# Four blocks of a graph layer begun ahead of the branch that chooses its form

## The chip, the cores and the metric

The kernel runs on one core of one Trainium2 chip. A core has a matrix engine (TensorE, PE in the profile, with its weight loads as PEld), a vector engine (VectorE, DVE), a scalar engine (ScalarE, ACT), a general engine (GpSimd, POOL) and a sync engine (SyncE, SP) that issues the transfers here. Each engine has its own queue of instructions and takes them in order; semaphores make one wait for another. Transfers bring data from memory (HBM) to the on-chip buffer (SBUF), and matmuls write to a small accumulator memory of eight banks (PSUM), which VectorE and ScalarE can read. The metric is the device time of one execution in microseconds.

## The reference

Four graph layers follow each other on 3327 nodes with 64 features; all use the same dense 3327 x 3327 adjacency, and after each comes a residual addition and a layer normalisation:

```python
x = _layernorm(x + _L0_gnn_ref(x, adj, L0_gnn_W), axis=-1)               # mean of neighbours, then a matmul
x = _layernorm(x + _L1_gnn_ref(x, adj, L1_gnn_weight, L1_gnn_bias), axis=-1)  # hyperbolic: see below
x = _layernorm(x + _L2_gnn_ref(x, adj, L2_gnn_W, L2_gnn_b), axis=-1)     # mean with itself, matmul, relu, unit norm
x = _layernorm(x + _L3_gnn_ref(x, adj, L3_gnn_weight, L3_gnn_bias), axis=-1)  # rank of each neighbour weights it
```

Layer 1 needs a value for every pair of nodes:

```python
w = adj / deg
log_ij = _logmap(x[:, None, :], x[None, :, :], c)
agg = jnp.einsum('ij,ijc->ic', w, log_ij)
transformed = agg @ weight + bias
```

Layer 3 weights a neighbour by its rank in the row (a running count of the nonzero entries), so those ranks must be counted from the adjacency somewhere.

## The kernel before

The nodes are padded to 3328: 26 blocks of 128 source nodes (NB) by four chunks of 832 target nodes (CH), taken in the order 0, 3, 1, 2 (ORDER). The adjacency is stored transposed and comes in pairs of blocks, 128 x 2 x 832 numbers, 832 KB, into four buffers in turn (`load_adj`, L274, issued by SP). A chunk has 13 pairs.

Layer 0 (L626 to L745) goes through each chunk's pairs from 12 down to 0. `aggregate_pair` (L434, matmul at L439) adds a pair to the chunk's sums in one PSUM bank. For three of the four chunks the ranks for layer 3 are counted on the way: `Ranks.mask` (L457) makes a 0/1 mask on VectorE (L459), and `count` (L496) sums it along the nodes with three groups of four matmuls (L505) into two PSUM pairs and lets ScalarE write the ranks (L515). The counts of a pair need a row from the pair before: `carry` (L483) takes it from that pair's result and subtracts it in the mask (L491, VectorE). So counts wait in a list, and `left` (L711) says how many stay in it: three in the last two chunks. What is left is counted after the last pair (L740).

At the end of a chunk `keep_sums` (L424) copies the sums to SBUF, `sums0` (L542) transposes them (L549) and takes degree, mean and residual on VectorE, and `features0` (L572) makes the normalised features xr, their scaled form xu, and a doubled copy `twice` (POOL) that `transposes0` (L611) turns into the operands ut and wt of layer 1. For three chunks this is done beside the next chunk's pairs, step by step (`side`). For the last one only `sums0` is, and `features0` is left for layer 1 (`late`).

Layer 1 has two forms. The short one (`layer1_far`) holds if no node lies near the origin; it is chosen at run time. Each chunk notes its near nodes; at the end VectorE adds them up (`nearest`, L742), a one-element matmul gives the count (the vote, L744), VectorE writes it as an integer (`n_near`, L745), and every engine loads it and branches (L1369, L1371). PSUM is handed over there: layer 0's pool of tiles is closed and each arm opens its own.

`layer1_far` (L785) takes 104 steps, one for each block in each chunk. `far_v` (L789) makes two matmuls (L793) into one of three PSUM pairs; `far_factors` (L801) computes p from it and the adjacency on VectorE (L804) and a square on ScalarE, then a product of both: either ScalarE, ScalarE, POOL (L817, L818, L819, form G) or ScalarE, VectorE (L809, L812, form V), in the pattern GVGGGV. `far_aggregate` (L822, L824) multiplies the result s with xu into the chunk's sums, six steps behind (L1_AHEAD). Groups of two steps are issued together: two `far_v`, their factors, then two aggregations. From step 3 on (LATE_AT) one step of the last group's `features0` is put behind each block's p, and then its transposes.

The first two adjacency pairs of layer 1 have a place of their own: the buffer `sums`, whose halves are free once the groups in them are transposed. SP issues both loads after all of layer 0's pairs (L734).

TensorE's order is written out by hand: `issue_after` puts an instruction behind another in the program order without making it wait; where no such order is given, the framework's scheduler orders each engine's program.

Of the kernel before, what the change touches and what calls it, by code (L numbers as in the profile page):

```python
# [79 lines left out]


# [15 lines left out]
LATE_AT = 3  # L97
# [11 lines left out]
def four_gnn_layers_kernel(  # L109
# [516 lines left out]
    with ExitStack() as l0s:  # L626
# [60 lines left out]

        heads = {12: (24, 26), 11: (20, 24), 9: (13, 20), 6: (6, 13), 2: (0, 6)}
# [5 lines left out]
        for n, c in enumerate(ORDER):  # L694
# [4 lines left out]
            for jp in reversed(range(NB // 2)):  # L699
# [11 lines left out]
                left = (L0_SPILL - jp // 2 if ranks else jp // 2) if n < 2 else L0_LAG  # L711
# [3 lines left out]
                if side is not None and jp < NB // 2 - 1:  # L715
                    on_array = jp == NB // 2 - 2
                    if not step(side, (counted or issued) if on_array else mask if ranks else None):
                        side = None
                        transposes0(ORDER[n - 1], places.free(), counted or issued, True)
                        if n == NCH - 1:  # L720

                            nc.scalar.activation(nothing, wt[:, GROUPS[ORDER[n - 1]][0] * P].unsqueeze(1), AF.Tanh)
# [6 lines left out]
            if n < NCH - 1:  # L729
                side = finish0(c, banks.one(n % 2))  # L730
            else:
                last_group = all_of(sums0(c, banks.one(n % 2)))

        first_pairs = [  # L734
            load_adj(ORDER[0], PAIRS[k], sums[:, bass.ts(k, 2 * CH)].rearrange(
                "p (b i) -> p b i", b=2
            ))
            for k in range(2)
        ]
        count(masked, places, 0, counted)  # L740
        nearest = small.tile([P, 1], FP, name="nearest", tag="nearest")
        nc.vector.tensor_reduce(nearest, near, axis=AX.X, op=ALU.add)  # L742
        vote = banks.one(NCH % 2)
        nc.tensor.matmul(vote[0:1, 0:1], lhsT=nearest, rhs=ones, start=True, stop=True)  # L744
        nc.vector.tensor_copy(n_near, vote[0:1, 0:1])  # L745
# [39 lines left out]
    def layer1_far(banks, begin2):  # L785

        with tc.tile_pool(name="l1w", bufs=1) as wp:

# [105 lines left out]
            for start in range(0, total + L1_AHEAD, L1_GROUP):  # L894
                group = range(start, start + L1_GROUP)
                made = []
                for i in group:
                    if i < total:
                        if i % 2 == 0:
                            c, jp, a2 = next(pairs)  # L900
                        jb = 2 * jp + i % 2
                        v, v_issued = far_v(c, jb, summed)
                        made.append((i, jb, v, a2[:, i % 2, :]))
# [38 lines left out]
                for i in group:  # L942
                    n, j = divmod(i - L1_AHEAD, NB)
# [485 lines left out]
```

## Time and profile before

| | us |
|---|---|
| median of 3 runs | 538.31 (537.72 to 540.17) |
| the profiled execution, its own time | 536.65 |
| its span, first to last instruction | 534.9 |
| TensorE, VectorE, ScalarE, POOL busy | 484.1, 389.5, 334.1, 176.2 |
| last aggregation of layer 0 (pair 0), start | 141.84 |
| n_near written | 152.21 |
| first layer 1 matmul, first layer 1 aggregation | 153.88, 165.50 |
| last aggregations of layer 1 end, about | 345.9 |

The profile shows one execution. Times in it count from its first instruction. Each line of a time line is a run of equal instructions on one engine: start, time from the first start to the last end, engine, line of the source, operation, what is written and read, the size, how many, and in brackets how long the engine stood idle before it and which instruction ended the wait. An adjacency pair's aggregation is eight rows of L439, since every fp32 matmul leaves two rows; a block's `far_v` is four rows of L793.

### The profile page before, as it was taken

Reading aid. Unit: us, or ns where it says so; the run is one execution under the profiler, and the core shown is the slowest. Engines: PE = TensorE matmul, PEld = TensorE weight load, DVE = VectorE, ACT = ScalarE, POOL = GpSimd, SP = SyncE. Lnnn points to the kernel's source line nnn. Section 1 sums busy time; section 2 is a strip of 40 time slices with the busy share of each in tenths; the row PEclk is TensorE's granted clock in tenths of the full one; section 3 lists DMA queues with packets and bytes.
Section 4 is the critical chain, followed back from the end, with each engine's and each line's share of the span. In section 5 each row is a group of like instructions: output and inputs, shape, how many; then the busy total and the mean of one; then the engine's idle time right before and its main releaser. Section 6 shows DMA issues by size and latency. Waiting matters only on the chain.

```text
span 534.9 us, 8471 instructions
## 1 busy us (share of the span) xinstructions
PE 484.1 (90%) x3256; PEld 242.7 (45%) x3256; DVE 389.5 (73%) x707; ACT 334.1 (62%) x393; POOL 176.2 (33%) x150
## 2 busy tenths in 40 slices
PE   5999999998858999998999999997798999999993
PEld 3555444454423334433443353352344675656672
DVE  3575449899669888799789869945699972736834
ACT  1436536786868989788879977500278653236931
POOL 2001101112008888767767875221022020210000
PEclk9999999999989999999999999999999999999997
DMA  8899999899266777767767876879997789980012
GB/s 271 308 363 347 394 399 387 297 317 305 82 229 219 254 257 260 247 208 242 244 201 256 255 227 244 290 227 355 349 320 263 234 288 325 309 319 2 1 28 43
DMA packets 47172, 135.93 MB, mean 254 GB/s; under 512 B 6903, under 2 KB 7007, under 8 KB 47059
## 3 DMA queue, kind: packets, MB, share of 16 engines
q1 hardware_dynamic: 46594, 134.75, 73.6%
q0 software_dynamic: 384, 0.52, 0.4%
q8 instruction: 27, 0.44, 0.4%
q14 instruction: 23, 0.18, 0.1%
q10 hardware_dynamic: 144, 0.03, 0.0%
HBM read 134.27 MB, written 0.85 MB: 253 GB/s over the span
## 4 chain that ended last, share of the span: by engine, by line
PE 49%; DVE 27%; ACT 10%; DMA 6%; issue 3%; POOL 1%; ACTq 0%; POOLq 0%; DVEq 0%
PE one L439 14%; PE two L1263 10%; DVE p L804 7%; PE two L793 6%; DMA adj<-in_adjt_dram 6%; DVE mask L491 5%; PE one L824 5%; PE two L505 5%; DVE s L812 4%; DVE mask L459 3%; ACT s L817 3%; PE two L439 2%; ACT s L818 2%; ACT rank L515 2%; PE two L1187 1%
## 5 line engine op out<-in xcount | busy, mean ns | idle before, releaser
L819 POOL TENSOR_TENSOR s<-s,p 128x832 f32<-128x832 f32 x67 | 130.1, 1956 | 73.3 <-ACT s L818 61.4
L804 DVE SCALAR_TENSOR_TENSOR p<-two,adj 128x832 f32<-128x832 f32 x100 | 101.0, 1018 | 17.8 <-issue 13.3
L793 PE MATMUL two<-uw 64*128 64x416 f32 x416 | 90.1, 545 | 14.3 <-DVE s L812 7.2
L515 ACT ACTIVATE rank<-two,last_bias 128x832 uint8<-128x832 f32 x78 | 71.6, 952 | 45.5 <-DVE mask L491 22.8
L824 PE MATMUL one<-s,xu 128*64 128x416 f32 x416 | 85.2, 524 | 0.0
L439 PE MATMUL one<-adj,x0w 128*64 128x416 f32 x416 | 82.3, 523 | 2.3 <-ACT x0w L644 1.4
L817 ACT ACTIVATE s<-two,far_bias 128x832 f32<-128x832 f32 x67 | 63.7, 950 | 22.7 <-DVE p L804 20.7
L439 PE MATMUL one<-adj,xr 128*64 128x416 f32 x312 | 73.3, 515 | 3.1 <-DMA adj<-in_adjt_dram 3.1
L491 DVE SCALAR_TENSOR_TENSOR mask<-two,minus_last,mask 32x832 bf16<-32x832 f32 x48 | 52.5, 1093 | 24.4 <-PE two L505 20.0
L459 DVE TENSOR_SCALAR mask<-adj 128x1664 bf16<-128x1664 f32 x52 | 55.3, 1066 | 18.8 <-DMA adj<-in_adjt_dram 18.2
L793 PEld LDWEIGHTS two<-uw 64*128 64x128 f32 x416 | 37.5, 189 | 67.0 <-PE one L824 22.6
L1263 PE MATMUL two<-bits,parts 128*64 128x416 bf16 x624 | 67.7, 339 | 0.0
L505 PE MATMUL two<-mask,tri 128*64 128x416 bf16 x416 | 53.5, 346 | 10.9 <-DVE mask L491 8.3
L818 ACT ACTIVATE s<-s 128x832 f32<-128x832 f32 x67 | 60.1, 897 | 1.9
L1263 PEld LDWEIGHTS <-parts 128*64 128x64 bf16 x624 | 41.9, 110 | 20.4 <-issue 5.0
L824 PEld LDWEIGHTS one<-s,xu 128*64 128x64 f32 x416 | 25.8, 136 | 47.5 <-issue 46.6
L505 PEld LDWEIGHTS <-tri 128*64 128x64 bf16 x416 | 24.6, 110 | 45.9 <-issue 24.9
L439 PEld LDWEIGHTS one<-adj,x0w 128*64 128x64 f32 x416 | 29.4, 138 | 34.1 <-issue 23.5
L812 DVE SCALAR_TENSOR_TENSOR s<-two,p 128x832 f32<-128x832 f32 x37 | 37.6, 1016 | 3.0 <-ACT two L809 2.5
L439 PEld LDWEIGHTS one<-adj,xr 128*64 128x64 f32 x312 | 29.4, 137 | 22.4 <-issue 13.6
L1243 ACT ACTIVATE bits<-rank 128x1664 uint16<-128x1664 uint8 x21 | 32.3, 1579 | 9.9 <-PE two L1263 9.8
L809 ACT ACTIVATE two<-two,far_bias 128x832 f32<-128x832 f32 x37 | 34.0, 919 | 5.1 <-DVE p L804 4.9
(235 smaller groups left out, 453.0 us busy)
## 6 DMA issues: line engine op xcount, KB each, us to landing
adj<-in_adjt_dram SPq DMA_DIRECT2D x152, 832.0 KB, 5.6
sums<-in_adjt_dram SPq DMA_DIRECT2D x2, 832.0 KB, 6.0
uw<-in_adjt_dram SPq DMA_DIRECT2D x2, 832.0 KB, 6.5
uw<-in_xt_dram SPq DMA_DIRECT2D x1, 640.0 KB, 10.7
last_a<-in_adjt_dram POOLq DMA_DIRECT2D x4, 84.5 KB, 7.4
out_dram<-o SPq DMA_DIRECT2D x1, 224.0 KB, 3.7
uw<-in_xt_dram SPq DMA_DIRECT2D x1, 192.0 KB, 3.2
out_dram<-o SPq DMA_DIRECT2D x1, 192.0 KB, 2.3
```

What stands on the lines that cost most here:

```text
L439: issued = nc.tensor.matmul(acc[h * D : (h + 1) * D, 0:HC], lhsT=x[:, 2 * jp + k, 0:D], rhs=a2[:, k, bass.ts(h, HC)], start=(first and k = ...
L459: issued = nc.vector.tensor_scalar(mask, a2, 0.0, None, op0=ALU.not_equal)
L491: nc.vector.scalar_tensor_tensor(halves(last), ranks.after[P - 32 : P, :, 0:HC], minus_last[P - 32 : P, :], halves(last), op0=ALU.mult, op ...
L505: issued = nc.tensor.matmul(counts[k][rows, h, 0:HC], lhsT=lhsT[:, rows], rhs=mask[:, of, bass.ts(h, HC)], start=lhsT is tri, stop=(k == 1 ...
L515: nc.scalar.activation(halves(ranks.rank[:, 2 * jp + k, :]), counts[k][:, :, 0:HC], AF.Relu, bias=last_bias,)
L793: issued = nc.tensor.matmul(v[:, h, 0:HC], lhsT=wt[rows, bass.ts(jb, P)], rhs=ut[rows, bass.ds(c * CH + h * HC, HC)], start=True, stop=True,)
L804: issued = nc.vector.scalar_tensor_tensor(halves(p), v, 0.25 - 0.5 * FD, halves(a), op0=ALU.add, op1=ALU.mult)
L817: nc.scalar.activation(halves(s), v, AF.Square, bias=far_bias, scale=-2.0)
L818: nc.scalar.activation(s, s, AF.Copy, bias=FG)
L819: nc.gpsimd.tensor_mul(s, s, p)
L824: issued = nc.tensor.matmul(acc[h * D : (h + 1) * D, 0:HC], lhsT=xu[:, jb, 0:D], rhs=s[:, bass.ts(h, HC)], start=first, stop=last,)
L1263: issued = nc.tensor.matmul(acc3[c][h * D : (h + 1) * D, 0:HC], lhsT=parts[:, 2 * jp + b, bass.ts(part, D)], rhs=bits[:, b, bass.ts(h, HC) ...
```

## The change

Three things change.

1. In the last chunk of layer 0 fewer counts wait: `left` falls from 3 to 2 at pair 4 and to 1 at pair 1, so two counts move ahead of the last pairs and one is left for the end.
2. The first four blocks of layer 1 (L1_THERE) are begun in layer 0. The first `sums` load is issued behind pair 2's load. Block 0's matmuls follow the last pair; its p goes in place over the adjacency in `sums` (VectorE), and Square, Copy and product run on ScalarE and POOL. Block 1 follows the transposes of the last group, and its p stands behind `nearest` on VectorE, ahead of the `n_near` copy. The matmuls of blocks 2 and 3 stand behind the vote, and their p and s (form V) behind the `n_near` copy, ahead of each engine's branch.
3. In `layer1_far` steps 0 to 3 make nothing and only queue the finished blocks. Blocks 0 to 3 are aggregated in steps 4 to 7, none in 8 and 9, and from step 10 on the order is as before. `LATE_AT` becomes 4. The ScalarE table load for Tanh is tied to pair 4 and another operand.

The blocks' arithmetic is the same.

```diff
+L1_THERE = 4
...
-LATE_AT = 3
+LATE_AT = 4
...
+        first_pairs = []
+        first_s = l0.tile([P, CH], FP, name="first_s")
+
+        def load_first(k):
+            there = sums[:, bass.ts(k, 2 * CH)].rearrange("p (b i) -> p b i", b=2)
+            return load_adj(ORDER[0], PAIRS[k], there)
+
+        def first_v(k, place, behind):
+            jb = 2 * PAIRS[k // 2] + k % 2
+            for h in range(2):
+                rows = slice(h * D, (h + 1) * D)
+                issued = nc.tensor.matmul(
+                    place[:, h, 0:HC], lhsT=wt[rows, bass.ts(jb, P)],
+                    rhs=ut[rows, bass.ds(ORDER[0] * CH + h * HC, HC)], start=True, stop=True,
+                )
+                issue_after(issued, behind)
+            return issued
+
+        def first_p(k, place, behind):
+            a = halves(first_pairs[k // 2][:, k % 2, :])
+            issued = nc.vector.scalar_tensor_tensor(
+                a, place[:, :, 0:HC], 0.25 - 0.5 * FD, a, op0=ALU.add, op1=ALU.mult
+            )
+            if behind is not None:
+                issue_after(issued, behind)
+
+        def first_aside(k, place):
+
+            nc.scalar.activation(
+                halves(first_s), place[:, :, 0:HC], AF.Square, bias=far_bias, scale=-2.0
+            )
+            nc.scalar.activation(first_s, first_s, AF.Copy, bias=FG)
+            a = first_pairs[0][:, k, :]
+            nc.gpsimd.tensor_mul(a, first_s, a)
...
-                left = (L0_SPILL - jp // 2 if ranks else jp // 2) if n < 2 else L0_LAG
+                if n < 2:
+                    left = L0_SPILL - jp // 2 if ranks else jp // 2
+                else:
+                    left = L0_LAG if n == 2 else min(L0_LAG, (jp + 4) // 3)
+                if n == NCH - 1 and jp == 2:
+                    first_pairs.append(load_first(0))
+                if n == NCH - 1 and jp == 0:
+                    places_v = [places.zero()]
+                    issued = first_v(0, places_v[0], issued)
+                    first_p(0, places_v[0], mask)
+                    first_aside(0, places_v[0])
                 counted = count(masked, places, left, issued)
...
-                        if n == NCH - 1:
-
-                            nc.scalar.activation(nothing, wt[:, GROUPS[ORDER[n - 1]][0] * P].unsqueeze(1), AF.Tanh)
+                if n == NCH - 1 and jp == 4:
+
+                    b0 = GROUPS[ORDER[n - 1]][0]
+                    nc.scalar.activation(nothing, om[:, b0 : b0 + 1], AF.Tanh)
...
-        first_pairs = [
-            load_adj(ORDER[0], PAIRS[k], sums[:, bass.ts(k, 2 * CH)].rearrange(
-                "p (b i) -> p b i", b=2
-            ))
-            for k in range(2)
-        ]
-        count(masked, places, 0, counted)
+        first_pairs.append(load_first(1))
+        places_v.append(places.zero())
+        issued = first_v(1, places_v[1], counted)
+        counted = count(masked, places, 0, issued)
         nearest = small.tile([P, 1], FP, name="nearest", tag="nearest")
-        nc.vector.tensor_reduce(nearest, near, axis=AX.X, op=ALU.add)
+        issued = nc.vector.tensor_reduce(nearest, near, axis=AX.X, op=ALU.add)
+        first_p(1, places_v[1], issued)
+        first_aside(1, places_v[1])
         vote = banks.one(NCH % 2)
-        nc.tensor.matmul(vote[0:1, 0:1], lhsT=nearest, rhs=ones, start=True, stop=True)
-        nc.vector.tensor_copy(n_near, vote[0:1, 0:1])
+        voted = nc.tensor.matmul(vote[0:1, 0:1], lhsT=nearest, rhs=ones, start=True, stop=True)
+        issue_after(voted, counted)
+        known = nc.vector.tensor_copy(n_near, vote[0:1, 0:1])
+
+        places_v += [places.zero(), places.one()]
+        for k in (2, 3):
+            first_v(k, places_v[k], voted)
+            first_p(k, places_v[k], known)
+        for k in (2, 3):
+            v, a = places_v[k][:, :, 0:HC], halves(first_pairs[1][:, k % 2, :])
+            nc.scalar.activation(v, v, AF.Square, bias=far_bias, scale=-2.0)
+            nc.vector.scalar_tensor_tensor(a, v, FG, a, op0=ALU.add, op1=ALU.mult)
...
+            def summed_at(i):
+
+                if i < 2 * L1_THERE:
+                    return i - L1_THERE
+                return i - L1_AHEAD if i >= L1_THERE + L1_AHEAD else -1
...
+                        if i < L1_THERE:
+                            waiting.append((jb, a2[:, i % 2, :]))
+                            continue
...
-                    n, j = divmod(i - L1_AHEAD, NB)
+                    n, j = divmod(summed_at(i), NB)
```

## The prediction

> **What bounds the kernel now.** I read the page's busy shares and slices first (TensorE, PE, is busy 90% of the 534.9 us span), then the time line of each engine around the branch, since every edit lies between 117 and 180 us of the trace. TensorE's line there:
>
> ```profile
> 128.62 1.56 PE L439 MATMUL one<-adj,x0w 128*64 128x416 f32 x8
> ...
> 130.85 0.54 PE L505 MATMUL two<-mask,tri 128*64 128x416 bf16 x4 [0.31 <-DVE mask L491]
> ...
> 134.03 1.56 PE L439 MATMUL one<-adj,x0w 128*64 128x416 f32 x8
> ...
> 138.31 1.62 PE L439 MATMUL one<-adj,x0w 128*64 128x416 f32 x8
> ...
> 141.84 1.59 PE L439 MATMUL one<-adj,x0w 128*64 128x416 f32 x8
> ...
> 151.98 0.19 PE L744 MATMUL one<-ones,nearest 128*1 128x1 f32 x2
> 153.88 3.92 PE L793 MATMUL two<-uw 64*128 64x416 f32 x12 [1.71 <-ACT rank L515]
> ...
> 165.50 1.62 PE L824 MATMUL one<-s,xu 128*64 128x416 f32 x8
> ```
>
> L439 x8 is one adjacency pair's aggregation; 141.84 is pair 0, the last of layer 0, 128.62 is pair 4. L744 is the vote, the first L793 is layer 1, the first L824 its first aggregation. So from the end of layer 0's aggregation to the start of layer 1's, 143.2 to 165.5, TensorE is half idle. The first L793 waits not for the vote but for the last ScalarE (ACT) rank, which still reads layer 0's PSUM.
>
> VectorE's (DVE) line of the same stretch:
>
> ```profile
> 134.15 1.03 DVE L459 TENSOR_SCALAR mask<-adj 128x1664 bf16<-128x1664 f32 x1 [1.17 <-DMA adj<-in_adjt_dram]
> ...
> 145.64 0.17 DVE L552 COPY deg<-one 128x7 f32<-128x7 f32 x1
> ...
> 151.34 0.18 DVE L742 TENSOR_REDUCE nearest<-near_nodes 128x1 f32<-128x26 f32 x1
> 152.21 0.14 DVE L745 CAST n_near<-one 1x1 int32<-1x1 f32 x1 [0.69 <-PE one L744]
> 155.85 1.02 DVE L804 SCALAR_TENSOR_TENSOR p<-two,sums 128x832 f32<-128x832 f32 x1 [3.49 <-PE two L793]
> ...
> 162.54 1.02 DVE L804 SCALAR_TENSOR_TENSOR p<-two,adj 128x832 f32<-128x832 f32 x1 [0.56 <-POOL s L819]
> ```
>
> n_near is known at 152.35. L804 at 155.85 is block 0's p, the one at 162.54 is block 4's: the first block that the change leaves to layer 1. And the stretches' clock (columns: length, busy time and count of PE, PEld, DVE, ACT, POOL, then granted clock, DMA share, GB/s):
>
> ```profile
> 150.20:153.60 3.40, 1.08 (x12) 0.45 (x10) 1.40 (x4) 2.78 (x4) 0.00 (x0) 1.00 0.00 0
> 153.60:157.00 3.40, 3.12 (x10) 1.85 (x12) 1.02 (x1) 0.22 (x2) 0.00 (x0) 0.51 0.71 252
> 200.00:337.00 137.00, 130.06 (x678) 54.75 (x676) 117.15 (x192) 116.76 (x140) 101.97 (x53) 1.00 0.72 238
> ```
>
> After a stretch with 1.08 us of matmul in 3.40 the clock is halved for one such stretch; it made the first twelve L793 take 3.92 us where four take 0.97 (2.9 for twelve), so about 1.0 us is lost already before. In the last row layer 1's body has TensorE busy 95%: a start-up gained or lost is carried to the end.
>
> **What the skill says.** "TensorE: Matmul & The Clock Gate", Part 1: the clock is set by a free-running window of 3413 ns, and one idle window halves it; the two rows agree in the length, and show that 1.08 us busy in 3.40 still counts as idle. "PSUM — Partial Sum Buffer", PSUM bank collisions: two engines may not touch one bank together, reads included, so accesses are ordered; agrees: rank L515 is released by DVE L491, at 148.72 right at its end. "DMA: Bandwidth & Descriptors", Anatomy of one DMA: about 2 us fixed plus the bytes, stated for the GpSimd path; the SP loads here agree: an 832 KB load issued alone at 164.59 landed after 4.2 us, at some 405 GB/s 2.1 of it data.
>
> **The change, part by part** (trace times before; ' for after; order of instructions as the built program has it).
>
> 1. *Counts lag less.* Pairs 4 and 1 are each followed by two counts instead of one, so one count is left for the end instead of three. A count is three groups of 0.35 = 1.05 of TensorE, but a second one right behind needs the row that DVE carries from the first. Pair 4: first count done 131.74, DVE mask to 131.85, carry L491 131.88-132.97, so the second's last two groups run 133.03-133.73. Pair 3' starts at 133.73 against 131.57, pair 2' at 136.18 against 134.03: +2.15. Then pair 1': before it lost 0.41 and 0.18 to a mask that came late from DMA (134.15); now the mask is covered, so 1.05 of count and 0.9 of transposes bring it to 139.53 against 138.31: +1.22. Then two counts, waiting for L624 on ACT (to 142.38) and a carry (143.34-144.43): pair 0' starts at 145.19 against 141.84: **+3.35**.
>
> 2. *The tail.* Before, DVE's chain from deg (145.64) to nearest (151.52) holds two carries of 1.12: without them 3.64. After: pair 0' done 146.76, sums copies on DVE then ACT to 147.92, behind the last in-loop rank; TensorE has block 0's matmuls (0.8) and the left count (1.05) ahead of the transposes, 148.50-149.05. DVE has p of block 0 (1.02) and a carry (1.09) to 149.80. nearest' is there at 153.44. p of block 1 (1.02) stands ahead of the n_near copy: n_near' at 154.61 against 152.35, **+2.26**. So the lag edit does not bring the vote forward: it moves two counts ahead of the last pair, where each costs more than the two carries save. Beside the vote, block 1's p costs 1.16 against the wait of 0.69.
>
> 3. *Blocks 0 to 3 ahead of the branch.* After n_near' DVE does p of block 2 (154.67-155.69), block 3 (its matmuls wait in PSUM for block 1's Square on ACT, to 155.44, so 156.50-157.52), then the two s (each behind a Square of 0.93): to 159.57. Only then does DVE load the flag and branch; SP takes 1.00 for that (152.35 to its issue at 153.35), so 160.57. TensorE's first layer 1 matmul, block 4's, waits for the whole PSUM pool of layer 0, so for that last s: 159.6, done 160.6; block 5's matmuls and the first aggregations, whose inputs have long been ready, are queued behind it (161.2-162.75). POOL's products of blocks 0 and 1 end by 158.3, under DVE's. Block 4's adjacency is issued by SP at n_near' + 1.0 = 155.61; four loads queue there, 0.5 apart; before, the second landed 7.5 after its own issue, so 8.0 after the first's, and the first is one data time of 2.1 ahead of it. Its landing lies between 4.2 (as when alone) and 5.9 after its issue: 159.8 to 161.5. So p of block 4 starts at 160.6 to 161.5; I take 161.0. Before: 162.54. Four blocks' p, s, Squares and POOL products are gone from the ramp, yet it starts **1.5** earlier only, because 2.26 was lost before the vote, and the same DVE work (6 ops of 1.0) stands ahead.
>
> 4. *From block 4 to full speed.* The same chain of p, s and features0 of the last group (LATE_AT 4: now behind block 4's p, which was behind block 1's s). On DVE, each p or s 1.02, each dependent small op 0.2: p of block 4 from 161.0, of 5 to 163.0, four small ops, p of 6 from 163.75 (its load lands at n_near' + 9.0 = 163.6, as before), p of 7 from 165.1 (its matmuls wait for block 4's Square and stand behind the first aggregations), s of 5 to 167.1. Block 8's matmuls wait for that s, as it holds their PSUM pair: p of 8 from 168.1, s of 7 to 170.1, p of 9 to 171.0, 0.9 of small ops, p of 10 to 172.9, xu 173.45. TensorE: blocks 10 and 11 wait for the s of 7, 170.1-171.7; aggregation of 4 and 5 at 171.7 against 172.96: -1.3. But features0 lies later among the blocks: xu is written at 173.45 (before 173.03), and POOL's copy of it (0.94) stands behind block 9's product (173.0-174.95), so to 175.9. TensorE, through with its next matmuls at 174.9, waits for it, then has 0.6 of transposes: aggregation of 6 and 7 at 176.5 against 176.76: **-0.3**.
>
> 5. *Clock.* In the old run the halved stretch is in these times. Now TensorE has only block 3's matmuls between 154.5 and 159.6, so a window with under 1 us of matmul falls there and the half clock comes between 156 and 161, over block 4's matmuls and the first aggregations: 0 if it falls early, 1.6 if whole. I take **+1.0**.
>
> 6. *Costed at nothing.* The table load (1.28) moves from 141.95 to about pair 6, where ACT idled 1.87 before a rank; with that cover gone it costs 1.3, and at its old place it ended with a carry, at 143.2, so at most 0.2 is won. The first sums load passes two adjacency loads on SP: up to 2.1 later for pair 1's mask, which DVE reaches at 135.05 against 134.13 of landing; bounds 0 and 1.2, I take 0, since DMA had room at 128-130 us. Removing 4 x 0.8 of L793 from layer 1 gains nothing more, as DVE and ACT set the ramp.
>
> Sum: -0.3 + 1.0 = +0.7. The profiled execution took 536.65, so 537.4 for a like one; the runs' median is 538.31, 1.66 above it, and I predict 538.31 + 0.7 = **539.0 us**: no change within 0.5% (2.7 us, about what a measurement of this kernel can tell).
>
> **Rivals.** *Slower*: the half clock lasts two windows, because the ramp keeps TensorE only some 60% busy (3.53 in 5.10 and 1.77 in 3.40 in the old ramp). Each whole window costs up to 1.7 of TensorE's work, so -0.3 + 3.4 = +3.1: 541.4. It decides if the clock is still 0.5 past 162 us. For it: over 3 us of idle TensorE at 156.3-159.6. Against: before, one stretch was enough. *Faster*: the added counts cost only their 2.1 of matmul, and old stalls (0.41, 0.18, 0.85) absorb 1.4 of it, so pair 0' is 0.7 late instead of 3.35, n_near' 0.4 early, p of block 4 4.2 early, and 1.3 is given back at POOL; with no halved clock 538.31 - 2.9 = 535.4. It decides if pair 0' is less than 1 late. Against it: the carry between back-to-back counts is a true dependency (1.51 and 0.89 were waited for it between the last three counts before). *The change does not do what it says*: block 0 could be ordered behind the counts; the built order has it directly after the last pair, so no more than 0.03 for it, at 538.3.
>
> **Chances.** Forecast 0.68 (own range 537 to 541), slower rival 0.18, faster 0.11, ineffective 0.03. Range for 8 in 10: 535.9 to 541.8, which holds the clock's 0 to 1.6, the 0.9 of landing and 1.2 of the mask. The ineffective case gives 0.02 to within and 0.01 to faster: faster 0.12, within 0.70, slower 0.18.
>
> **What would show it.** The last L439-like aggregation 3 us later (step 1); n_near 2 us later (2); first layer 1 matmul released by DVE's last s and p of block 4 within 1 us of 161 (3); a wait of TensorE for POOL ahead of the first transposes of layer 1 (4); 0.5 clock after 156 us (5). The forecast is wrong if n_near comes no later than 152.5, or if the clock stays low.

## The result and the profile after

The changed kernel takes **544.75 us** (median of 4 runs, 543.48 to 545.47) against 538.61 for the kernel before on the same chip: a ratio of 1.0108, 95% interval 1.0078 to 1.0139. It is 6.1 us slower; the forecast was 539.0, with a range up to 541.8.

Lines of the changed kernel have new numbers: aggregation of layer 0 L441, counts L507, near_nodes L563, block 0 to 3's matmuls L702, their p L711, GpSimd's product of blocks 0 and 1 L724, nearest L788, the vote L792, n_near L794, s of blocks 2 and 3 L803; in layer 1 the matmuls L857, p L868, ScalarE's part of s L881, aggregation L888, transposes L619.

Executions differ by up to some 4 us in layer 0 ahead of pair 4's aggregation, where nothing was edited, so all times "behind pair 4" below count from the start of that aggregation in the same execution (128.62 before, 130.52 after). TensorE's time line of the kernel after, with the lines that answer to those shown of before:

```profile
130.52 1.56 PE L441 MATMUL one<-adj,x0w 128*64 128x416 f32 x8
...
147.20 1.56 PE L441 MATMUL one<-adj,x0w 128*64 128x416 f32 x8
...
156.69 0.19 PE L792 MATMUL one<-ones,nearest 128*1 128x1 f32 x2 [2.17 <-DVE nearest L788]
156.81 3.62 PE L702 MATMUL two<-uw 64*128 64x416 f32 x8
163.74 3.10 PE L857 MATMUL two<-uw 64*128 64x416 f32 x8 [3.31 <-DVE sums L803]
166.77 1.62 PE L888 MATMUL one<-sums,xu 128*64 128x416 f32 x8
...
175.71 2.03 PE L857 MATMUL two<-uw 64*128 64x416 f32 x8 [2.20 <-ACT s L881]
177.67 2.91 PE L888 MATMUL one<-s,xu 128*64 128x416 f32 x8
...
182.85 0.63 PE L619 MATMUL one<-ident,twice 128*128 128x128 f32 x4 [0.67 <-DVE scale L605]
183.41 1.62 PE L888 MATMUL one<-s,xu 128*64 128x416 f32 x8
```

In the kernel before, blocks 4 and 5 and then blocks 6 and 7 were aggregated here:

```profile
172.96 1.62 PE L824 MATMUL one<-s,xu 128*64 128x416 f32 x8
...
176.69 1.62 PE L824 MATMUL one<-s,xu 128*64 128x416 f32 x8
```

Pair 0 (147.20) starts 16.68 behind pair 4; before it was 13.22. The eight rows of L702 and of L857, 1.67 at full clock, take 3.62 and 3.10. Layer 1's first aggregation comes 36.25 behind pair 4 (before 36.88), so at that point the change is even a little ahead; but blocks 4 and 5 are aggregated at 47.15 behind it (before 44.34) and blocks 6 and 7 at 52.89 (before 48.07). From pair 4 to the end of the span it is 412.2 against 406.3: 5.9, the size of the whole loss, and 4.8 of it are there when blocks 6 and 7 are aggregated. Blocks 0 to 3 are finished early, and then the pipeline of layer 1 has to be filled anew from block 4.

VectorE and GpSimd (POOL) in the same stretch, the second fence from GpSimd's own time line:

```profile
155.25 1.17 DVE L563 SCALAR_TENSOR_TENSOR near_nodes<-ss_last,real 128x7 f32<-128x7 f32 x1
...
157.48 0.14 DVE L794 CAST n_near<-one 1x1 int32<-1x1 f32 x1
...
161.49 2.11 DVE L803 SCALAR_TENSOR_TENSOR sums<-two,sums 128x832 f32<-128x832 f32 x2
165.69 1.02 DVE L868 SCALAR_TENSOR_TENSOR p<-two,adj 128x832 f32<-128x832 f32 x1 [2.10 <-PE two L857]
...
177.15 1.49 DVE L592 TENSOR_SCALAR xu<-var 128x7 f32<-128x7 f32 x1
```

```profile
154.04 2.36 POOL L724 TENSOR_TENSOR sums<-first_s,sums 128x832 f32<-128x832 f32 x1 [23.43 <-ACT first_s L722]
...
176.66 3.88 POOL L883 TENSOR_TENSOR s<-s,p 128x832 f32<-128x832 f32 x2 [2.37 <-DVE p L868]
```

Two VectorE operations on 7 numbers per lane took 1.17 and 1.49 us. Before, the same two took 0.17 and 0.16:

```profile
151.14 0.17 DVE L561 SCALAR_TENSOR_TENSOR near_nodes<-ss_last,real 128x7 f32<-128x7 f32 x1
...
172.16 0.16 DVE L590 TENSOR_SCALAR xu<-var 128x7 f32<-128x7 f32 x1
```

In the changed kernel the first ends at 156.42, when GpSimd's product ends (156.40); the second at 178.64, when the first of the two products does (two in 3.88, so 178.60). The time line does not mark this as a wait: it shows only as a long duration. Not every small operation is held: a reciprocal of 7 numbers from SBUF (L591, at 176.91) took 0.20 beside the second product. The clock, from the stretches' view (columns as before: length, busy time and count of PE, PEld, DVE, ACT, POOL, granted clock, DMA share, GB/s):

```profile
149.60:153.02 3.42, 2.45 (x25) 1.39 (x23) 3.10 (x9) 2.91 (x4) 0.00 (x0) 1.00 0.19 18
153.02:156.43 3.41, 1.50 (x14) 0.59 (x12) 3.30 (x6) 2.74 (x4) 2.36 (x1) 1.00 0.60 237
156.43:159.84 3.41, 3.05 (x10) 1.09 (x10) 2.19 (x4) 2.02 (x3) 0.22 (x1) 0.50 0.11 15
159.84:163.25 3.41, 0.59 (x2) 0.00 (x0) 2.64 (x3) 1.69 (x2) 1.74 (x1) 0.50 0.91 351
163.25:166.67 3.42, 2.93 (x8) 1.27 (x8) 1.32 (x3) 0.00 (x0) 0.00 (x0) 0.50 1.03 409
...
173.49:176.91 3.42, 1.22 (x10) 0.73 (x8) 3.23 (x7) 2.13 (x3) 1.05 (x2) 1.00 0.55 217
176.91:180.32 3.41, 3.41 (x12) 0.77 (x8) 3.38 (x7) 2.23 (x3) 3.41 (x2) 0.50 0.75 237
```

Three windows in a row at half clock, then a fourth ten microseconds on; before there was one.

### The profile page after: what moved, and what is told of

It is laid out like the page before. It is cut to its first block, busy times and chain, and to the rows that moved or that the text cites. A ratio compares the mean times of both kernels' runs of the same rounds, so it can differ in the third digit from the quotient of the medians.

```text
span 542.7 us, 8469 instructions
## 1 busy us (share of the span) xinstructions
PE 487.2 (90%) x3256; PEld 242.4 (45%) x3256; DVE 391.9 (72%) x708; ACT 333.9 (62%) x392; POOL 174.7 (32%) x149
## 4 chain that ended last, share of the span: by engine, by line
PE 51%; DVE 28%; DMA 8%; ACT 8%; issue 3%; DVEq 0%; ACTq 0%
PE one L441 14%; PE two L1330 10%; DMA adj<-in_adjt_dram 8%; DVE p L868 7%; PE two L857 7%; PE one L888 6%; DVE mask L493 5%; PE two L507 4%; DVE mask L461 4%; DVE s L876 3%; ACT s L881 3%; PE two L441 2%; ACT s L882 2%; PE two L1254 1%; PE one L1345 1%
## 5 line engine op out<-in xcount | busy, mean ns | idle before, releaser
L883 POOL TENSOR_TENSOR s<-s,p 128x832 f32<-128x832 f32 x64 | 124.4, 1954 | 52.7 <-ACT s L882 39.8
L868 DVE SCALAR_TENSOR_TENSOR p<-two,adj 128x832 f32<-128x832 f32 x100 | 101.3, 1020 | 21.7 <-issue 14.5
L857 PE MATMUL two<-uw 64*128 64x416 f32 x400 | 86.9, 547 | 13.8 <-DVE s L876 6.9
L441 PE MATMUL one<-adj,x0w 128*64 128x416 f32 x416 | 82.5, 524 | 4.0 <-DMA adj<-in_adjt_dram 2.6
L888 PE MATMUL one<-s,xu 128*64 128x416 f32 x400 | 83.3, 532 | 0.0
L881 ACT ACTIVATE s<-two,far_bias 128x832 f32<-128x832 f32 x64 | 60.9, 951 | 26.9 <-DVE p L868 20.5
L441 PE MATMUL one<-adj,xr 128*64 128x416 f32 x312 | 73.4, 515 | 3.3 <-DMA adj<-in_adjt_dram 3.3
L857 PEld LDWEIGHTS two<-uw 64*128 64x128 f32 x400 | 36.1, 188 | 65.4 <-PE one L888 22.4
L507 PE MATMUL two<-mask,tri 128*64 128x416 bf16 x416 | 52.6, 345 | 9.6 <-DVE mask L493 7.8
L882 ACT ACTIVATE s<-s 128x832 f32<-128x832 f32 x64 | 57.4, 897 | 1.8
L888 PEld LDWEIGHTS one<-s,xu 128*64 128x64 f32 x400 | 25.2, 137 | 46.3 <-issue 45.3
L441 PEld LDWEIGHTS one<-adj,x0w 128*64 128x64 f32 x416 | 29.2, 138 | 36.1 <-issue 24.1
L507 PEld LDWEIGHTS <-tri 128*64 128x64 bf16 x416 | 24.2, 110 | 45.2 <-issue 25.1
L441 PEld LDWEIGHTS one<-adj,xr 128*64 128x64 f32 x312 | 29.4, 137 | 22.6 <-issue 13.5
```

Of the source, the lines that this page charges most:

```text
L441: issued = nc.tensor.matmul(acc[h * D : (h + 1) * D, 0:HC], lhsT=x[:, 2 * jp + k, 0:D], rhs=a2[:, k, bass.ts(h, HC)], start=(first and k = ...
L507: issued = nc.tensor.matmul(counts[k][rows, h, 0:HC], lhsT=lhsT[:, rows], rhs=mask[:, of, bass.ts(h, HC)], start=lhsT is tri, stop=(k == 1 ...
L857: issued = nc.tensor.matmul(v[:, h, 0:HC], lhsT=wt[rows, bass.ts(jb, P)], rhs=ut[rows, bass.ds(c * CH + h * HC, HC)], start=True, stop=True,)
L868: issued = nc.vector.scalar_tensor_tensor(halves(p), v, 0.25 - 0.5 * FD, halves(a), op0=ALU.add, op1=ALU.mult)
L881: nc.scalar.activation(halves(s), v, AF.Square, bias=far_bias, scale=-2.0)
L882: nc.scalar.activation(s, s, AF.Copy, bias=FG)
```

## The experiments

Theory: three things lose the time, the halved clock (three windows and one more), a later vote, and VectorE's waits for GpSimd. Rivals: the lag edit alone; or the early blocks by the order that they force on the ramp, whatever the clock and GpSimd do. Each run was timed beside the kernel before; ratios are to it, with 95% intervals.

### The two edits apart

The changed kernel with the old lag:

```diff
-                    left = L0_LAG if n == 2 else min(L0_LAG, (jp + 4) // 3)
+                    left = L0_LAG
```

> The changed kernel with the old lag of three counts in layer 0's last chunk; blocks 0 to 3 stay ahead of the branch. Theory (lag): the lag edit delays the last aggregation of layer 0 by 3.4 us and the vote by about 2, so pair 0's aggregation comes back to 13 to 14 us behind pair 4's (16.7 in the changed kernel), n_near to 24 to 25.5 us behind it (27.1), and the time falls by 1.5 to 3, to 542 to 543. Rival (clock): the time is lost to half-clock windows behind the vote alone; n_near may come earlier, but three or more halved windows remain and the time stays at 543.5 to 545.5.

Measured: 546.94, ratio 1.0156 (1.0117 to 1.0195), 2.2 slower than the changed kernel. The last pair did come back, to 12.38 behind pair 4, but n_near came later (28.97), since two counts and their carries now stand around the vote: VectorE's copy of n_near waited 1.81 for the vote, which TensorE has behind the last count. Five windows in a row were at half clock. Both theories missed: beside the early blocks the lag edit helps.

The lag edit alone, in the kernel before (the same line the other way round):

> The kernel before with only the lag edit: no block of layer 1 ahead of the branch. Theory (lag): pair 0's aggregation 3.4 us later, less the two carries (2.2) that leave the tail, so n_near about 1.2 later and the time 538.6 + 1 to 1.5, at 539.5 to 540.2, with one halved window as before. Rival (lag harmless or useful): the vote comes no later and the time is 537 to 538.6. Rival (clock): the tail's idle spreads differently and a second window is halved: 541 or more.

Measured: 540.14, ratio 1.0038 (1.0015 to 1.0061), so about 2 slower; one halved window; pair 0 at 16.67 behind pair 4, n_near at 24.52 (before 23.73). As the lag theory said, if a little dearer. Alone it does not bring the vote forward. The two edits do not add up: by the ratios the lag edit alone costs 2.0 us, the early blocks with the old lag 8.4, both together 5.8. So the early blocks bring most of the loss, and the lag edit softens it.

### GpSimd's product out of the way of the vote

```diff
+        seen = small.tile([P, 1], FP, name="seen", tag="seen")
+        first_product(first_a, nc.gpsimd.tensor_copy(seen, nearest))
         first_p(1, places_v[1], issued)
```

> The changed kernel with GpSimd's product of block 0 ordered behind nearest (GpSimd first copies nearest, which it has to wait for). Theory (port): the product runs from 154.0 to 156.4 beside VectorE's near_nodes, which has two SBUF inputs and took 1.17 us instead of 0.17; with the product behind it near_nodes takes 0.17 to 0.2, nearest and n_near come 1.0 earlier (26.1 us behind pair 4 instead of 27.1), and the time falls by 0.5 to 1.2, to 543.6 to 544.3. Rival (the long near_nodes is a chance of that one execution, for instance a late instruction fetch): it is short or long in either kernel and the time stays within 0.4 of the changed kernel's.

Measured: 544.20, ratio 1.0114 (1.0077 to 1.0152), no different from the changed kernel. Yet the mechanism is there:

```profile
153.85 0.17 DVE L563 SCALAR_TENSOR_TENSOR near_nodes<-ss_last,real 128x7 f32<-128x7 f32 x1
...
155.08 0.14 DVE L800 CAST n_near<-one 1x1 int32<-1x1 f32 x1
```

```profile
156.41 0.95 ACT L719 ACTIVATE first_s<-two,far_bias 128x832 f32<-128x832 f32 x1 [1.80 <-POOL sums L726]
```

In VectorE's line near_nodes takes 0.17 again and n_near comes 26.1 behind pair 4 instead of 27.1. In ScalarE's line the gain is gone at once: block 1's square has to wait for the moved product, which still reads the one buffer `first_s`. Block 4's p stayed at 35.3 behind pair 4, and three windows were halved here too. The rival, a chance of one execution, is out: where the product stayed, near_nodes took 1.16 to 1.19 us in five other traces, and 0.17 only with the old lag, where a carry stands ahead of it until the product is over. The Trainium skill, "SBUF — State Buffer", section "Who interferes with whom", has the rule that fits: VectorE with two SBUF inputs contends with a GpSimd instruction that reads SBUF, and whichever issues second is fully blocked. near_nodes has two such inputs (1.17 against 0.17). For the xu column, with one input from SBUF, that section says a `tensor_scalar` can also take the shared port, under conditions; the trace agrees as far as two like operations with their input in PSUM (L589, L590) took 0.17 and 0.16 beside the same product.

The kernel before showed it already, had the question been asked. VectorE, then GpSimd:

```profile
160.89 1.09 DVE L396 TENSOR_SCALAR var<-ss_last 128x7 f32<-128x7 f32 x1
```

```profile
160.00 7.70 POOL L819 TENSOR_TENSOR s<-s,p 128x832 f32<-128x832 f32 x4 [31.29 <-ACT s L818]
```

Seven numbers per lane in 1.09 us, up to 161.98, about where the first of four products ends (160.00 + 7.70/4 = 161.93). The length follows the product: in two runs further down the same operation took 0.80 us (the kernel before with wasted matmuls) and the xu column 0.89 (the late features twice as fast), and each ended within 0.05 us of a product.

### The clock held up by wasted matmuls

A helper `fill` puts fp32 matmuls of x0w with itself into PSUM that nobody reads: first four ahead of the vote and seven behind block 3's matmuls.

```diff
+        counted = fill(banks.one(NCH % 2), 4, counted)
         vote = banks.one(NCH % 2)
...
+        fill(banks.one(1), 7, v_issued)
```

> The changed kernel with matmuls that compute nothing wanted: four (0.39 us each at full clock) between the last count and the vote, seven behind block 3's matmuls, ahead of the branch, all into PSUM that nobody reads afterwards. Theory (clock): no window from 152 to 164 is idle any more, the clock stays at 1.0 through that stretch, block 2's and 3's matmuls take 1.7 us instead of 3.6 and block 4's and 5's 1.9 instead of 3.1, p of block 4 comes 2 us earlier behind n_near, and the time falls by 2 to 4, to 541 to 543. Rival (chain of VectorE and ScalarE sets the ramp whatever the clock): the time stays within 1 of the changed kernel's 544.75. Rival (the windows are halved for another reason than idle TensorE): the clock is still 0.5 from 156 to 166.

Measured: 542.98, ratio 1.0096 (1.0057 to 1.0134). No halved window before 175, as meant, but a wasted matmul took 0.73 us, twice what was planned, so they held up the vote and block 4 (p at 36.3 behind pair 4). The scheduler had also put block 2's matmuls ahead of block 3's. Again with two and four, and with the changed kernel's order:

```diff
+        counted = fill(banks.one(NCH % 2), 2, counted)
...
-        for k in (2, 3):
-            first_v(k, places_v[k], voted)
+        v_issued = voted
+        for k in (3, 2):
+            v_issued = first_v(k, places_v[k], v_issued)
             first_p(k, places_v[k], known)
+        fill(banks.one(1), 4, v_issued)
```

> As the run with eleven wasted matmuls, which took 0.73 us each and so stood in the way of the vote (0.3) and of block 4 (1.9): now two before the vote (154.5 to 156.0, done ahead of nearest) and four (2.9 us) behind block 2's matmuls, with block 3's first as in the changed kernel. Theory (clock costs the ramp): the clock is 1.0 from 152 to 166, block 3's matmuls take 0.97 instead of 1.8, the last s before the branch ends 1.0 earlier behind n_near and block 4's p starts 2.0 earlier behind n_near (6.1 instead of 8.1); time 541.5 to 543. Rival (the ramp is set by the chain of VectorE, ScalarE and the late features of the last group, which the clock hardly touches): block 4's p comes 1 to 2 earlier, but the third aggregation pair does not, and the time stays within 1 of 544.75.

Measured: **541.97**, ratio 1.0068 (1.0040 to 1.0096), 2.8 below the changed kernel, and no halved window at all. TensorE:

```profile
158.11 0.97 PE L702 MATMUL two<-uw 64*128 64x416 f32 x4
159.88 0.97 PE L702 MATMUL two<-uw 64*128 64x416 f32 x4 [0.80 <-ACT first_s L719]
160.78 3.01 PE L729 MATMUL one<-x0w 128*64 128x416 f32 x8
164.16 1.67 PE L870 MATMUL two<-uw 64*128 64x416 f32 x8 [0.37 <-DVE sums L816]
```

Block 4's p comes 6.5 behind n_near instead of 8.1, and blocks 6 and 7 are aggregated at 50.58 behind pair 4 instead of 52.89. Six more matmuls make the kernel faster, so the halved clock does cost time. How much is less sure: the ratios differ by 2.2 us, give or take 2.3, and in the traces blocks 6 and 7 gain 2.3. More than half of the loss is left, so the clock is not all.

### The late features twice as fast

```diff
-                    if late is not None and i >= LATE_AT and not step(late, p_issued):
+                    for _ in range(2):
+                        if late is not None and i >= LATE_AT and not step(late, p_issued):
```

> The changed kernel, with two steps of the last group's features per block instead of one, from block 4 on as before. Theory (late features): in the changed kernel these steps begin 2.6 us later behind block 4's p than in the kernel before, xu of the last group is written 13.9 us behind that p instead of 9.9, and the transposes that wait for GpSimd's copy of it hold the aggregation of blocks 6 and 7 (17.7 behind p instead of 14.2). With two steps a block xu is written about 10 behind p, the transposes no longer wait, aggregation of 6 and 7 is 1.5 to 2.5 earlier and the time 542.2 to 543.2. Rival (VectorE is full in the ramp, so what the features gain the p's lose): 544 to 546.

Measured: 544.82, ratio 1.0110 (1.0079 to 1.0140): nothing gained, as the rival said. xu was written 9.8 behind block 4's p as planned, but the transposes moved ahead of blocks 10 and 11 in TensorE's queue and stopped it there:

```profile
177.00 0.63 PE L619 MATMUL one<-ident,twice 128*128 128x128 f32 x4 [3.21 <-DVE scale L605]
```

The line also corrects the expectation: the transposes wait for VectorE's last small step `scale`, which still reads the PSUM bank that they write into, not for GpSimd's copy.

### Two blocks ahead of the branch instead of four

```diff
-L1_THERE = 4
+L1_THERE = 2
```

with LATE_AT back to 3 and blocks 2 and 3 left to layer 1.

> The changed kernel with two blocks ahead of the branch instead of four (blocks 2 and 3 are made in layer 1 as before, late features from block 3 on). Theory (the branch drains the pipeline: block 4 waits for the last s of block 3, which the order puts 6.0 us behind n_near): layer 1's first matmuls come 1.0 to 1.5 behind n_near instead of 6.1, block 4's p 4 to 5 behind it instead of 8.1, and the time falls by 2 to 4, to 541 to 543. Rival (the early blocks are work done in time that was idle anyway, only the half clock costs): as many or more halved windows, block 4's p no earlier than 7 behind n_near, time 544 to 546.

Measured: 541.11, ratio 1.0041 (1.0021 to 1.0061), 3.6 below the changed kernel; two halved windows instead of four. Layer 1's first matmuls came 1.1 behind n_near instead of 6.1, but VectorE's first p there only 4.1 behind it:

```profile
163.01 1.96 DVE L860 SCALAR_TENSOR_TENSOR p<-two,sums 128x832 f32<-128x832 f32 x2 [4.07 <-POOL sums L724]
```

It waits for GpSimd's product of block 1, still at work ahead of the branch. So two early blocks lose less than four, though part of that may be the two windows fewer at half clock, and the branch does act as a drain: what is begun ahead of it has to be finished before the next stage can start.

### Both ports mended, without and with the clock held

The product behind nearest, now with a second buffer for block 1's factors, and the column of xu on ScalarE:

```diff
-        nc.vector.tensor_scalar_add(xu[:, b0:b1_, 0], inverse, -0.5)
+        if aside:
+            nc.vector.tensor_scalar_add(xu[:, b0:b1_, 0], inverse, -0.5)
+        else:
+            nc.scalar.activation(xu[:, b0:b1_, 0], inverse, AF.Copy, bias=-0.5)
```

> The changed kernel with both places mended in which a small VectorE operation stood behind a GpSimd product: GpSimd's product of block 0 is ordered behind nearest, with a buffer of its own for the factors of block 1 (in the run that moved only the product, ScalarE then waited 1.8 us for that buffer), and the one column of xu that VectorE wrote in 1.49 us instead of 0.16 is written by ScalarE. Theory (port): near_nodes takes 0.17, n_near comes 1.0 earlier (26.1 us behind pair 4), xu of the last group 1 to 1.3 earlier behind block 4's p, and the third aggregation pair (blocks 4 to 7 are the third and fourth) comes 1 to 2.3 earlier; time 542.3 to 543.7. Rival (these waits are covered by the half clock and by the order of TensorE's queue): within 0.6 of 544.75.

Measured: 541.07, ratio 1.0048 (1.0025 to 1.0071), 3.7 below the changed kernel, more than the theory gave. Part of it may be clock: this execution has one halved window (162.8 to 166.2) instead of four. n_near is 26.1 behind pair 4.

With the short fill as well:

> Both mended ports together with the six wasted matmuls of the short fill. Theory (the loss is the sum of half clock, 2.4 to 2.8, and of the two waits for the port, 2.3): what is left over the kernel before is under 1.5, so 538.5 to 540. Rival (the early blocks cost by themselves, by the order of the ramp behind the branch): the time stays at 541 or more, as with the short fill alone (541.97).

Measured: **539.00**, ratio 1.0011 (0.9991 to 1.0031): no longer told apart from the kernel before. On top of the mended ports the fill gains 2.0 by the ratios, give or take 1.6. The rival in its size, 541 or more, is out: half clock and shared port together are nearly all of the loss. That the early blocks also lose something by themselves is not excluded: the interval leaves up to 1.7 us, and in this trace, which has one halved window in the ramp, blocks 6 and 7 are still aggregated 1.6 later than in the trace of before.

Which of the two ports it is: each of the two edits alone, with the clock held by the short fill (its six matmuls as shown):

> The short fill (six wasted matmuls, 541.97), and only the column of xu written by ScalarE; GpSimd's product of block 0 stays where it delays near_nodes. If VectorE's wait for the port at xu carries to the end, xu of the last group comes 1.0 to 1.3 earlier behind block 4's p and the time falls by 0.9 to 1.4, to 540.6 to 541.1. If TensorE's transposes are set by something else (GpSimd's copy behind two products, which end when they end), nothing changes: 541.6 to 542.4, and the 3.0 that both mended ports gained belong to the vote.

> The short fill, and only GpSimd's product of block 0 behind nearest (with its second buffer of factors); the column of xu stays on VectorE. If the vote's delay carries to the end in full, n_near is 26.1 behind pair 4 instead of 27.1, block 4's p 1.0 to 1.1 earlier (32.5 behind pair 4), and the time falls by 0.9 to 1.2, to 540.8 to 541.1. If the port at the vote is all of what both mended ports gained: 539 to 539.6.

Measured: 541.79, ratio 1.0066 (1.0045 to 1.0087), for the xu column alone, and 540.36, ratio 1.0028 (1.0007 to 1.0049), for the product alone, beside 541.97 for the fill without either. Product first: 1.6, of which n_near shows 1.0 (26.1 against 27.1 behind pair 4) and block 4's p 1.1 (32.5 against 33.6). The xu column: 0.2 alone, 1.4 on top of the product (to 539.00). In the trace with the column mended the gain was eaten by one halved window, from 174.1 to 177.5:

```profile
173.69 2.81 PE L873 MATMUL two<-uw 64*128 64x416 f32 x8 [2.20 <-ACT s L897]
```

Block 10's p then waits 1.27 for TensorE where VectorE waited for GpSimd. Two runs from above had no halved window at this place: the one that only moved the product, and the one with both ports mended. Block 10's p in each:

```profile
178.03 1.01 DVE L874 SCALAR_TENSOR_TENSOR p<-two,adj 128x832 f32<-128x832 f32 x1
```

```profile
176.70 1.02 DVE L878 SCALAR_TENSOR_TENSOR p<-two,adj 128x832 f32<-128x832 f32 x1 [0.17 <-PE two L867]
```

The first is 3.03 behind block 9's p (175.00), with the column on VectorE, the second 1.89 (174.81), with the column on ScalarE. So the column is worth 1.1 us in the trace where no halved window falls there, and nothing where one does. In time each of these differences is known to some 1.5 to 2 us: the vote's port is shown by time and trace, the xu column by the trace alone.

### Is there a better version?

Two wasted matmuls in the kernel before, behind its vote:

```diff
+        fill(banks.one(1), 2, voted)
```

> The kernel before with two wasted matmuls (0.73 us each) behind the vote, in the 1.7 us in which TensorE waits for the last rank. Theory (clock): the window from 150.2 to 153.6 is then 2.5 us busy instead of 1.05 and the next one is not halved; the first twelve matmuls of layer 1 take 2.9 instead of 3.9, block 0's p is 0.9 earlier, and the time falls by 0.5 to 1, to 537 to 537.5. Rival (the start of layer 1 is set by something else, or the window still counts as idle): 537.7 to 538.5.

Measured: 537.45, ratio 0.9995 (0.9972 to 1.0018). The trace shows the mechanism (no halved window, first twelve matmuls in 2.37 where they took 3.92, blocks 6 and 7 aggregated at 46.26 behind pair 4 against 48.07, of which 0.8 is the earlier pair 0 of this execution, 12.39 behind pair 4 against 13.22), but the gain is not told apart from nothing. With a fifth buffer for p and the last group's variance on ScalarE besides:

```diff
-                p = wp.tile([P, CH], FP, name="p", tag="p", bufs=4)
+                p = wp.tile([P, CH], FP, name="p", tag="p", bufs=5)
```

> The kernel before with the two wasted matmuls behind the vote, a fifth buffer for p (block 4's p waited 0.56 for a GpSimd product to free one) and the variance of the last group on ScalarE (on VectorE it took 1.09 us instead of 0.16, up to the end of a GpSimd product). Theory (port and clock): block 4's p comes 1.0 to 1.5 earlier still than with the wasted matmuls alone (161.0), the time is 536 to 537.2. Rival (the ramp of the kernel before is set by GpSimd's products, one behind the other from 160 to 168): as with the wasted matmuls alone, 537.0 to 538.

Measured: 537.91, ratio 0.9984 (0.9960 to 1.0008); block 4's p at 32.3 behind pair 4, as with the fill alone (32.1): the rival's case.

Two early blocks with all of it mended: block 1's s on VectorE, block 0's product behind nearest, the xu column on ScalarE, five wasted matmuls.

```diff
+        nc.scalar.activation(v, v, AF.Square, bias=far_bias, scale=-2.0)
+        issued = nc.vector.scalar_tensor_tensor(a, v, FG, a, op0=ALU.add, op1=ALU.mult)
```

> Two blocks ahead of the branch, with block 1's s on VectorE (in the run with two blocks VectorE's first p behind the branch waited 4.1 us for GpSimd's product of block 1), the product of block 0 behind nearest, the column of xu on ScalarE and five wasted matmuls. Theory (fewer early blocks, no port, no half clock: nothing of the loss is left): n_near 26.1 behind pair 4, the first p behind the branch 3.0 to 3.5 behind n_near instead of 4.2, time 537.5 to 539.5, level with the kernel before. Rival (the early blocks lose to the kernel before by the later vote alone, 2.4 us of n_near): 540 to 541.

Measured: 537.59, ratio 0.9980 (0.9957 to 1.0003), 7.2 below the changed kernel and in no halved window. n_near is still 2.6 later behind pair 4 than before (26.3), and blocks 6 and 7 are aggregated 1.2 earlier (46.85); 0.8 of that is the late pair 0 in the trace of before. It is level with the kernel before or a little under it. Against four early blocks with both ports mended and the short fill (539.00) it is 1.7 faster by the ratios, give or take 1.7, so a small loss by the early blocks themselves is likely and not shown. None of the versions is shown to beat the kernel before.

The table puts the main runs together, from each one's own trace (us behind pair 4; windows at half clock between 140 and 195 us of it) and its runs:

| | n_near | block 4's p | blocks 6, 7 aggregated | halved windows | median |
|---|---|---|---|---|---|
| before | 23.7 | 33.9 | 48.1 | 1 | 538.61 |
| changed | 27.1 | 35.2 | 52.9 | 4 | 544.75 |
| + short fill | 27.1 | 33.6 | 50.6 | 0 | 541.97 |
| + short fill, product | 26.1 | 32.5 | 49.6 | 1 | 540.36 |
| + short fill, product, xu | 26.1 | 32.5 | 49.7 | 1 | 539.00 |
| two blocks, all mended | 26.3 | 32.6 | 46.9 | 0 | 537.59 |

## Why the prediction was wrong

Two terms failed. The clock (step 5) was priced at 1.0 us and cost about 2.3 in the trace. GpSimd's products were priced at nothing: in step 3 those of blocks 0 and 1 "end by 158.3, under DVE's", and step 4 counts its products only as delays of GpSimd's own copy. But a product stops small VectorE operations beside it, at the vote and again at the xu column, and these two stops cost about 2.2 in the trace.

**Step 1, the counts** (pair 0 later by 3.35): right, 3.46, for the execution that it was worked out on. That execution of before had lost some 0.8 to a transfer there that others did not lose (pair 0 at 12.4 behind pair 4 in three other runs with the old lag), so the price is rather 4.3, and alone the edit costs about 2 us in time. That it doesn't bring the vote forward is right; that it helps once blocks stand in the tail was not seen.

**Step 2, the tail** (n_near later by 2.26): 3.37. The working leaves out GpSimd: its products were taken as hidden by running beside VectorE. The product of block 0 does run beside it, and so blocks near_nodes, 1.0 us ahead of the vote. With that mended n_near is 26.1 behind pair 4, where the step had 26.0.

**Step 3, block 4 at 161.0** (1.5 earlier than before; 32.4 behind pair 4): 35.2, that is 1.25 later than before. What releases it was right, VectorE's last s (3.31 of waiting at 163.74). 1.1 of the miss is step 2's, 1.6 the clock (33.6 with the short fill alone); with both mended it is 32.5.

**Step 4, the ramp** (blocks 6 and 7 earlier by 0.3): later by 4.8. Of the miss, 2.8 is carried in from step 3. Of the rest, 1.1 is the second port, as the pair of runs above shows, and 0.6 the third halved window, which reaches into the first aggregations: from block 4's p to block 6's it is 3.64, with the short fill 3.00. The fourth window costs only 0.1: from block 10's p to the aggregation of blocks 6 and 7 it is 4.79, with the short fill 4.70. The wait ahead of the transposes came, but its cause was misnamed: VectorE's last feature step, not GpSimd's copy.

**Step 5, the clock** (1.0; bounds 0 and 1.6): mis-sized. The step let the half clock fall once, over one window, "0 if it falls early, 1.6 if whole", and gave its length to a rival with 0.18. Three windows fell there. Against the trace with the short fill they hold block 4's p back by 1.6 and blocks 6 and 7 by 2.3; in time the fill gains 2.2 by the ratios, to within some 2. The slower rival had the course right, and its point of decision came out so: the clock was still at 0.5 past 162. Its 3.4 for the size is about as far off on the other side. What argued against it, one stretch had been enough before, does not hold, as 156.43 to 159.84 shows: 3.05 us busy of 3.41, and the next window is halved again.

**Step 6** held: the table load fell into the gap between two ranks, and no mask of the last pairs waited for a transfer.

The sum then, for blocks 6 and 7 in the trace: -0.3 of steps 1 to 4, 2.3 for the clock in place of 1.0, and 2.2 for the two stops by GpSimd, which no step had, make 4.2 of the 4.8 measured; 0.6 is not placed. In time the medians put 2.8 on the clock and 3.0 on the stops, but each is known only to some 2. The range ended 3 short; the stops were in none of the cases.

## What to carry to other kernels

Work moved into another engine's idle time isn't hidden by that alone: here a GpSimd product held small VectorE operations on SBUF until it ended, though not all of them, and the one that matters may be seven numbers ahead of a vote. A profile shows such a stop as a long duration, not as a wait, so compare the shortest and the longest time of one small operation before giving work to GpSimd. And where TensorE is thin on both sides of a barrier, price the halved clock for as long as it stays thin, not for one window; a few wasted matmuls, kept shorter than the wait they fill, are a cheap test of it.

## What the runs showed of the hardware

- The Trainium skill, "TensorE: Matmul & The Clock Gate", Part 1, says that an idle window halves the clock and a busy one restores it. The traces give the busy time that decides, as the profile counts it. In all sixteen, from 25 to 520 us, every window at full clock with up to 1.33 us of matmul in 3.41 was followed by a halved one, and none with 1.52 or more was; in between, 1.43 and 1.50 were, 1.44 and 1.47 were not. A halved window with up to 2.42 us busy never restored the clock. From 2.94 up most did, but one with 2.94 (old lag) and one with 3.05 (changed kernel) did not, while one with 2.93 (changed kernel, 163.25 to 166.67) did; what tells these apart was not found.
- Where these windows fall differs from one execution to the next: in the changed kernel the first halved one begins 0.3 us ahead of the vote, in the run with doubled features, the same up to the branch, 1.9 behind it. The same wait of 2.20 us for ScalarE in the ramp was followed by a halved window in five traces and by none in four. A price for the clock from one trace is therefore one draw.
- Four wasted fp32 matmuls (eight rows in the trace of the run with eleven) took 2.96 us, where the aggregation's four of the same size take 1.56. The aggregation's write to the two halves of the PSUM partitions in turn and the wasted ones all to one half; that the halves overlap is a likely reason, and was not tried. The wasted ones also change their weights every time, the aggregation's every second time.
- A VectorE operation that starts first holds GpSimd up in turn: the product of block 0 took 2.36 instead of 1.96; it began at 154.04, and VectorE's square of y, begun at 153.96, ran to 154.58. In the six other runs with the product at this place it took 2.34 to 2.38.
